# GAT layers with a residual layer norm: ScalarE's step tiles dealt anew in the first stage

## The chip, the cores and the metric

The kernel runs on one core of a Trainium2 chip. The time is the device time of one execution in microseconds (us). Five engines of the core run side by side, each through its own list of instructions in order, and wait for one another by semaphores: PE (TensorE, matrix products), DVE (VectorE), ACT (ScalarE), POOL (GpSimd) and SP (which here only starts transfers). The trace shows PE's weight loads apart, as PEld.

## The reference

Two graph attention layers on 512 nodes with 768 features, a residual and a layer norm. The graph has 16,896 edges (8,192 drawn pairs in both directions and a loop at each node), sorted by destination; an edge may occur more than once.

```python
def gat_layer(x, W, a_s, a_d, b, edge_index, concat):
    h = (x @ W).reshape(n, H, C)
    src, dst = (edge_index[0], edge_index[1])
    alpha_s = jnp.einsum('nhc,hc->nh', h, a_s)
    alpha_d = jnp.einsum('nhc,hc->nh', h, a_d)
    e = jax.nn.leaky_relu(alpha_s[src] + alpha_d[dst], NEG_SLOPE)
    m = jax.ops.segment_max(e, dst, num_segments=n)
    e = jnp.exp(e - m[dst])
    denom = jax.ops.segment_sum(e, dst, num_segments=n)
    alpha = e / (denom[dst] + EPS)
    msg = h[src] * alpha[:, :, None]
    out = jax.ops.segment_sum(msg, dst, num_segments=n)
...
h = gat_layer(x, W1, a_src1, a_dst1, b1, edge_index, concat=True)   # 8 heads
h = jax.nn.elu(h)
out = gat_layer(h, W2, a_src2, a_dst2, b2, edge_index, concat=True) # 1 head
return _layernorm(x + out)
```

## The kernel before

The kernel does not walk the edges. It counts them once, in `cnt`, a 512 x 512 table of how many edges lead from a source to a destination (and `absent`, a large negative number where there is none), and then does the attention of each head as dense 512 x 512 work. All large products are done in seven smaller ones of half the size instead of eight (the names `P1` to `P7`). The order of the instructions on every engine is written out by hand; no scheduler changes it.

**The first stage** (the first 63 us) does three things at once: the counting, the first projection `x @ W1` of head 0 (`first_projection`, fourteen products of three matmuls' depth, and the first four products of head 1), and the transposition of `x` on PE with copies of it by ACT (`turn_x`, line 205).

**The counting.** The edges are cut into 132 chunks of 128. For a chunk, DVE makes a narrow one-hot of the destinations within a block of 32 nodes (`od`, line 492, a quarter of the chunks at once), and one wide row per edge over all 512 sources (`os`, 128 x 512). A matmul of the two (line 542) adds the chunk to 32 rows of a counting tile in PSUM. The nodes make four tiles of 128 destinations. For three of them the wide row is a one-hot by DVE (line 516, `is_equal`). For tile `S = 2` it is a row of steps by ACT (line 514, the sign of `nodes - index`, with the negated index `nidx` as bias, which line 504 makes for all chunks): counting signs and taking the difference of neighbouring columns gives the same counts. That difference is the work of `counted_by_steps`: ACT reads the tile out of PSUM (lines 402 and 403), DVE subtracts (line 404), ACT makes `absent` (line 405). The other tiles are read out by `counted` (lines 395 and 396). A chunk on the border between tile 2 and its neighbour needs both kinds.

**The batches.** The chunks are dealt into nine batches, each with so many of the chunks outside tile 2 (`ours`) and so many inside it (`theirs`). The loop over the batches issues for batch n: DVE's one-hots (`sources`, with the subtractions of finished products in their middle, `waiting`), extra work (`extra`: the sums of x, the logits of head 0), then products until `wants[n]` are issued, each followed on ACT by the copy of its result (for products that only need a copy), by copies of `x` after the first and third product (`turns`), and by a `share` of the steps of batch n + 1 (`ahead`); and last the matmuls of batch n (`count`). The chunks of a batch go to four queues, one for each group of 32 rows, and are issued in turn; a few may stay over for the next batch. A tile whose chunks have all been counted is read out at the end of that `count`, before the next batch's instructions. After the last batch the logits are spread over the partitions by PE (`spread`), and the softmax of head 0 begins.

**The ring.** All wide rows, of DVE and of ACT, share the 32 buffers of `os`, given out in the order in which they are issued; an instruction that writes a buffer waits for the matmul that last read it.

The line numbers below are those of the kernel before; behind the first removed line the changed kernel's are one lower, and from the middle of the loop on two higher.

Of the kernel before, what the change touches and what calls it, by code (L numbers as in the profile page):

```python
# [13 lines left out]
AF = mybir.ActivationFunctionType  # L14
# [9 lines left out]
def kernel(tc: tile.TileContext, *args):  # L24


    with ExitStack() as ctx:
        flags = ctx.enter_context(tc.tile_pool(name="flags", bufs=1))
        ctx.enter_context(tc.manual_schedule())
        flag = flags.tile([1, 1], I32, name="flag")  # L30
        again = gat_pass(tc, flag, *args)
        with tc.If(again != 0):
            gat_pass(tc, None, *args)
# [3 lines left out]
def gat_pass(  # L37
# [16 lines left out]
    nc = tc.nc  # L54
# [145 lines left out]
    def turn_x(t, r):  # L200

        ps = mm.tile([P, 512], F32, name="mm")
        for k in range(HK):
            nc.tensor.transpose(ps[:, k * P:(k + 1) * P], x_sb[:, t, (r * HK + k) * P:(r * HK + k + 1) * P], ident)  # L204
        nc.scalar.copy(xT[:, r * HK:(r + 1) * HK, t * P:(t + 1) * P],
                       ps[:, :HALF].rearrange("p (k n) -> p k n", n=P))
# [4 lines left out]
    if general:  # L211
        nc.vector.tensor_copy(idx_f, idx_i)
        idx = ohp.tile([P, 2, EC], F32, name="idx")
# [6 lines left out]
    else:  # L220
# [41 lines left out]
        idx = ohp.tile([P, EC], F32, name="idx")  # L262
# [59 lines left out]
    def projection(h, XA, B_):  # L322

        HS[h] = hs = hpool.tile([P, NT, D], F32, name="hs")
        new_alpha(h)
        bank = {}
        tt = nc.vector.tensor_tensor

        def pair(p, i, start, empty):
            def multiply():  # L330
                if start:
                    bank[i] = mm.tile([P, 512], F32, name="mm")
                product(bank[i], XA, B_, p, i, start)
            return multiply, lambda: empty(i, bank[i][:, :HALF])

        steps = [
            ("P1", True, lambda i, ps: nc.scalar.copy(hs[:, 2 + i, L], ps)),
            ("P2", False, lambda i, ps: nc.scalar.copy(hs[:, i, L], ps)),
            ("P6", True, lambda i, ps: tt(hs[:, i, R], hs[:, 2 + i, L], ps, op=ALU.add)),
            ("P7", True, lambda i, ps: tt(hs[:, 2 + i, R], hs[:, i, R], ps, op=ALU.add)),  # L340
            ("P4", False, lambda i, ps: tt(hs[:, 2 + i, L], hs[:, i, R], ps, op=ALU.add)),
            ("P5", True, lambda i, ps: tt(hs[:, 2 + i, R], ps, hs[:, 2 + i, R], op=ALU.subtract)),
            ("P3", False, lambda i, ps: tt(hs[:, i, R], ps, hs[:, i, R], op=ALU.subtract)),
        ]
        return [pair(p, i, start, empty) for p, start, empty in steps for i in range(2)]
# [95 lines left out]
    def spread(h):  # L441
        pool, name = (bc, "bc") if h else (tr, "tr")
        BC[h] = pool.tile([P, 512], F32, name=name)
        for t in range(NT):
            nc.tensor.transpose(BC[h][:, t * P:(t + 1) * P],  # L445
                                AL[h][0][:, t:t + 1].to_broadcast([P, P]), ident)

    def lift(h, t):

        q = qpool.tile([P, N], F32, name="q")  # L450
        nc.scalar.activation(q, BC[h][:, :N], AF.Identity, bias=AL[h][1][:, t:t + 1], scale=-1.0)  # L451
        return q

    def leak(q):
        nc.vector.scalar_tensor_tensor(q, q, NEG_SLOPE, q, op0=ALU.mult, op1=ALU.min)

    def rank(q, t):

        nmax = small.tile([P, 1], F32, name="nmax")
        nc.vector.tensor_tensor_reduce(out=q, in0=q, in1=absent[:, t, :], scale=1.0, scalar=-NO_EDGE,  # L460
                                       op0=ALU.add, op1=ALU.min, accum_out=nmax)
        nc.scalar.activation(q, q, AF.Exp, bias=nmax, scale=-1.0)  # L462
        return q

    def turn_b1():
        psb = mm.tile([P, 512], F32, name="mm")
        nc.tensor.transpose(psb[:, :H * DC], b1_rows, ident[:H * DC, :H * DC])
        nc.scalar.copy(b1T, psb[:, :H * DC])
        nc.scalar.activation(nb1T, psb[:, :H * DC], AF.Copy, scale=-1.0)
# [4 lines left out]
    if not general:  # L474
# [15 lines left out]
        def destinations(lo, hi):  # L490
            lo, hi = at[lo], at[hi]
            nc.vector.tensor_tensor(od[:, lo:hi, :],  # L492
                                    rel[:, lo:hi].unsqueeze(2).to_broadcast([P, hi - lo, B]),
                                    nodes[:, :B].unsqueeze(1).to_broadcast([P, hi - lo, B]),
                                    op=ALU.is_equal)
# [5 lines left out]
            nc.vector.scalar_tensor_tensor(below, rel, 0.0, below, op0=ALU.is_ge, op1=ALU.mult, accum_out=found)  # L501

        nidx = ohp.tile([P, EC], F32, name="nidx")
        nc.scalar.activation(nidx, idx, AF.Copy, bias=0.5, scale=-1.0)

        def by_steps(b):
            return b * B // P == S
# [3 lines left out]
        def one_hot(c, steps):  # L511
            hot[c, steps] = o = ohp.tile([P, N], BF16, name="os", bufs=32)
            if steps:
                nc.scalar.activation(o, nodes, AF.Sign, bias=nidx[:, c:c + 1])  # L514
            else:
                nc.vector.tensor_scalar(o, nodes, idx[:, c:c + 1], None, op0=ALU.is_equal)  # L516

        def kinds(batch, steps):
            return [c for c in batch if any(by_steps(b) == steps for b in blocks[c])]

        def sources(chunks, between):

            for j, c in enumerate(chunks):
                if j == len(chunks) // 2:
                    for f in between:
                        f()
                one_hot(c, False)
# [37 lines left out]
        B1 = {}  # L565
        wants = [3, 4, 7, 10, 12, 14, 16, 18]
        batches = []
        for ours, theirs in ((16, 0), (8, 8), (8, 8), (12, 4), (12, 4), (12, 4), (13, 3), (14, 2), (4, 0)):
            take = [order[k][:m] for k, m in ((False, ours), (True, theirs))]
            del order[False][:ours], order[True][:theirs]  # L570
            batches.append(take[0][:ours // 2] + take[1] + take[0][ours // 2:])
        assert not any(order.values())
        pos, made, quarter, waiting = 0, set(), EC // NT, []
        for n, batch in enumerate(batches):
            for k in sorted({c // quarter for c in batch} - made):
                destinations(k * quarter, (k + 1) * quarter)
                made.add(k)
            sources(kinds(batch, False), waiting)
            ahead = kinds(batches[n + 1], True) if n + 1 < len(batches) else []
            items_here = max(wants[n] - pos if n < len(wants) else 0, 1)  # L580
            share = -(-len(ahead) // items_here)
            waiting = []
            for f in extra.pop(n, []):
                f()
            while n < len(wants) and pos < wants[n]:
                if pos == wholes:
                    pairs = projection(1, XA, B1)
                    items += [(m, e, False) for m, e in pairs[:4]]
                multiply, empty, on_vector = items[pos]
                multiply()  # L590
                if on_vector:
                    waiting.append(empty)
                else:
                    empty()
                pos += 1
                for t, r in turns.get(pos, []):
                    turn_x(t, r)
                for c in ahead[:share]:
                    one_hot(c, True)
                del ahead[:share]  # L600
            assert not ahead
            if n == 2:
                turn_b1()
            if n + 1 == len(batches):
                spread(0)
                q = [lift(0, t) for t in range(NT)]
                for t in range(NT - 1):
                    leak(q[t])
                for t in range(NT - 1):
                    rank(q[t], t)  # L610
            if n == 0:
                pst = mm.tile([P, 512], F32, name="mm")
                nc.tensor.matmul(pst[:1, :1], found, ones, start=True, stop=True)
            if n == 3:
                again = nc.values_load(flag[:1, :1], min_val=0, max_val=E)
            count(batch, n + 1 == len(batches))
# [460 lines left out]
```

## Time and profile before

| | |
|---|---|
| median of 4 runs | 653.74 us (653.34 to 654.59) |
| the profiled execution | 653.68 us, of which its span is 651.7 us |
| busy: PE, PEld | 640.9 us (98%), 398.3 us (61%) |
| busy: DVE, ACT, POOL | 506.9 us (78%), 273.8 us (42%), 49.0 us (8%) |
| mean granted clock of PE | 0.998 |
| wide one-hots by DVE, line 516 | 105, 344 to 354 ns each |
| rows of steps by ACT, line 514 | 39, 707 to 744 ns each |
| matmuls of the counting, line 542 | 210, 376 to 390 ns each, four groups side by side |

The span is the time from the first to the last instruction of the profiled execution. Instructions of an engine overlap a little at their ends, so the distance between the starts of two equal ones in a row is shorter than the length of one: sixteen one-hots of 0.35 us stand in 4.29 us. A matmul in fp32 is recorded as two.

The busy times by stretch of the first 82 us (us of the stretch in which each engine was busy):

| stretch, us | length | PE | DVE | ACT | granted clock |
|---|---|---|---|---|---|
| 0.00 to 21.66 | 21.66 | 19.60 | 17.61 | 15.39 | 1.00 |
| 21.66 to 42.73 | 21.07 | 20.77 | 19.00 | 13.88 | 1.00 |
| 42.73 to 59.70 | 16.97 | 16.97 | 16.73 | 8.71 | 1.00 |
| 59.70 to 62.73 | 3.03 | 2.16 | 2.36 | 2.26 | 1.00 |
| 62.73 to 82.00 | 19.27 | 19.27 | 17.63 | 13.57 | 1.00 |

### The profile page before, as it was taken

To read this page: it belongs to the slowest core of one execution; us is meant where nothing else is said; L and a number is where in the kernel's file an instruction comes from. 1 tells how busy PE (TensorE), PEld (TensorE's weight loads), DVE (VectorE), ACT (ScalarE), POOL (GpSimd) and SP (SyncE) were. 2 spreads that over 40 slices of the span, in tenths; PEclk is the share of its full clock that TensorE was granted. 3 is DMA by queue.
4 is the path that set the end of the run, shared out by engine and by line. 5 is a ranking of instruction groups with operands and counts; after the bars stand their busy time and mean duration, and the time that the engine had idled before them with its cause. 6 is when DMAs were issued, how large, how long until landed. Compare 5 with 4: busy or idle time off the path is not lost.

```text
span 651.7 us, 7058 instructions
## 1 busy us (share of the span) xinstructions
PE 640.9 (98%) x2347; PEld 398.3 (61%) x2347; DVE 506.9 (78%) x1102; ACT 273.8 (42%) x469; POOL 49.0 (8%) x90
## 2 busy tenths in 40 slices
PE   8999999999999999999999999999999999999995
PEld 5544586557755586557755586557755545645553
DVE  7989989968777777858777777858775588876775
ACT  6774744530736044531736054521736043243440
POOL 1320020011000010011000010011000000000000
PEclk9999999999999999999999999999999999999999
DMA  9993498196506790296506790296407865000122
GB/s 321 330 195 86 79 330 212 38 263 199 123 0 176 155 271 20 46 264 200 113 1 174 170 264 13 49 266 203 103 1 205 204 176 133 25 0 0 34 56 77
DMA packets 74186, 90.88 MB, mean 139 GB/s; under 512 B 36710, under 2 KB 58526, under 8 KB 74142
## 3 DMA queue, kind: packets, MB, share of 16 engines
q1 hardware_dynamic: 60478, 68.72, 33.6%
q0 software_dynamic: 12976, 20.65, 18.3%
q10 hardware_dynamic: 688, 0.98, 0.4%
q8 instruction: 20, 0.33, 0.2%
q14 instruction: 24, 0.20, 0.1%
HBM read 78.02 MB, written 1.57 MB: 122 GB/s over the span
## 4 chain that ended last, share of the span: by engine, by line
PE 96%; DVE 3%; issue 0%; ACT 0%; DVEq 0%
PE mm L304 64%; PE mm L763 17%; PE mm L709 6%; PE mm L1029 3%; PE held L304 2%; DVE os L516 1%; PE tr L542 1%; PE bc L177 1%; DVE odw L492 1%; PE bc L445 0%; PE bc L542 0%; PE tr L957 0%; PE tr L678 0%; PE mm L204 0%; DVE w1t L378 0%
## 5 line engine op out<-in xcount | busy, mean ns | idle before, releaser
L304 PE MATMUL mm<-w,gT 128*128 128x384 f32 x288 | 97.4, 487 | 0.0
L304 PE MATMUL mm<-w,xT 128*128 128x384 f32 x264 | 88.4, 488 | 0.0
L304 PEld LDWEIGHTS mm<-w,gT 128*128 128x128 f32 x288 | 53.9, 190 | 35.7 <-issue 2.0
L304 PEld LDWEIGHTS mm<-w,xT 128*128 128x128 f32 x264 | 49.8, 190 | 35.7 <-ACT os L514 0.8
L462 ACT ACTIVATE q<-q,nmax 128x512 f32<-128x512 f32 x36 | 25.8, 721 | 89.9 <-DVE nmax L460 89.9
L304 PE MATMUL mm<-w1t,gS 128*128 128x384 f32 x180 | 60.7, 486 | 0.0
L767 ACT COPY u<-mm 128x256 f32<-128x256 f32 x18 | 6.7, 372 | 119.3 <-PE mm L763 119.3
L304 PE MATMUL mm<-w2t,xS 128*128 128x384 f32 x168 | 56.6, 487 | 0.0
L763 PE MATMUL mm<-PT,hs 128*128 128x256 f32 x216 | 52.6, 379 | 0.0
L362 DVE TENSOR_TENSOR h<-h,mm 128x384 f32<-128x384 f32 x72 | 39.6, 551 | 14.4 <-PE mm L304 13.8
L304 PEld LDWEIGHTS mm<-w1t,gS 128*128 128x128 f32 x180 | 34.1, 190 | 23.6
L304 PEld LDWEIGHTS mm<-w2t,xS 128*128 128x128 f32 x168 | 31.8, 190 | 22.4 <-ACT q L451 0.4
L763 PEld LDWEIGHTS mm<-PT,hs 128*128 128x128 f32 x216 | 41.0, 190 | 7.2 <-issue 0.4
L686 ACT COPY nr<-q 128x1024 uint16<-128x1024 uint16 x32 | 33.4, 1044 | 23.2 <-DVE q L672 15.8
L709 PE MATMUL mm<-PT,hs 128*128 128x512 f32 x96 | 41.6, 593 | 0.0
L691 ACT COPY PT<-zr 128x1024 uint16<-128x1024 uint16 x32 | 37.1, 1159 | 2.0 <-DMA zr<-nr 2.0
L763 PE MATMUL mm<-pS,gS 128*128 128x256 f32 x144 | 37.1, 380 | 0.0
L304 PE MATMUL mm<-w,gS 128*128 128x384 f32 x96 | 32.6, 486 | 0.0
L304 PE MATMUL mm<-w1t,gT 128*128 128x384 f32 x96 | 32.5, 487 | 0.0
L304 PE MATMUL mm<-w,xS 128*128 128x384 f32 x96 | 32.5, 487 | 0.0
L106 POOL DMA_DIRECT2D w1t<-in_L_gnn_W_dram x7 | 8.9, 1267 | 312.5 <-PE mm L304 181.4
L709 PEld LDWEIGHTS mm<-PT,hs 128*128 128x128 f32 x96 | 18.2, 190 | 22.9 <-issue 21.5
(184 smaller groups left out, 1072.7 us busy)
## 6 DMA issues: line engine op xcount, KB each, us to landing
w<-in_L_gnn_W_dram SPq DMA_DIRECT2D x90, 384.0 KB, 6.1
w<-in_L_gnn_W_dram POOLq DMA_DIRECT2D x16, 576.0 KB, 9.7
w2t<-in_L_gnn_W_dram SPq DMA_DIRECT2D x10, 576.0 KB, 10.4
w1t<-in_L_gnn_W_dram SPq DMA_DIRECT2D x9, 576.0 KB, 4.4
w2t<-in_L_gnn_W_dram POOLq DMA_DIRECT2D x8, 576.0 KB, 10.0
w1t<-in_L_gnn_W_dram POOLq DMA_DIRECT2D x7, 576.0 KB, 8.5
a_s<-in_L_gnn_a_src_dram SPq DMA_DIRECT2D x8, 384.0 KB, 4.0
a_d<-in_L_gnn_a_dst_dram SPq DMA_DIRECT2D x8, 384.0 KB, 5.3
```

Of the source, the lines that this page charges most:

```text
L106: nc.gpsimd.dma_start(t1, upper[:, :, R], accum_op=ALU.add)
L177: nc.tensor.matmul(idle, zeros[:, :P], zeros, start=True, stop=True)
L304: nc.tensor.matmul(ps[:, :HALF], A_[p][:, k, i * P:(i + 1) * P], B_[p][:, k, :], start=start and k == 0, stop=k == HK - 1, skip_group_chec ...
L362: nc.vector.tensor_tensor(a, a, ps, op=ALU.subtract if p == "P7" else ALU.add)
L462: nc.scalar.activation(q, q, AF.Exp, bias=nmax, scale=-1.0)
L492: nc.vector.tensor_tensor(od[:, lo:hi, :], rel[:, lo:hi].unsqueeze(2).to_broadcast([P, hi - lo, B]), nodes[:, :B].unsqueeze(1).to_broadcas ...
L686: nc.scalar.copy(apart.rearrange("p (h n) -> p h n", h=2), q.bitcast(U16).rearrange("p (n h) -> p h n", h=2))
L691: nc.scalar.copy(PT.rearrange("p s n -> p (s n)").bitcast(U16).rearrange("p (s n h) -> p s n h", s=NT, h=2)[:, :, t * P:(t + 1) * P, :], p ...
L709: nc.tensor.matmul(ps[:, :N], HS[h][:, s, c * P:(c + 1) * P], PT[:, s, :], start=(s == 0), stop=(s == NT - 1))
L763: nc.tensor.matmul(bank[p][:, :HN], A_[p][:, k, c * P:(c + 1) * P], B_[p][:, k, :], start=over is None and k == 0, stop=k == 1, skip_group ...
L767: nc.scalar.copy(u, part("P1"))
L1029: nc.tensor.matmul(ps[:, :cols.stop - cols.start], PT[:, s, t * P:(t + 1) * P], h2[:, s, cols], start=(s == 2), stop=(s == 1))
```

## The change

```diff
@@ -501,7 +501,6 @@
         nidx = ohp.tile([P, EC], F32, name="nidx")
-        nc.scalar.activation(nidx, idx, AF.Copy, bias=0.5, scale=-1.0)
@@ -565,7 +564,7 @@
-        for ours, theirs in ((16, 0), (8, 8), (8, 8), (12, 4), (12, 4), (12, 4), (13, 3), (14, 2), (4, 0)):
+        for ours, theirs in ((16, 0), (8, 8), (8, 8), (12, 4), (12, 5), (12, 5), (13, 3), (14, 0), (4, 0)):
@@ -578,7 +577,7 @@
-            share = -(-len(ahead) // items_here)
+            share = len(ahead) // (items_here + 1) if n == 0 else -(-len(ahead) // items_here)
@@ -595,10 +594,13 @@
                 for t, r in turns.get(pos, []):
                     turn_x(t, r)
+                if pos == 1:
+                    nc.scalar.activation(nidx, idx, AF.Copy, bias=0.5, scale=-1.0)
                 for c in ahead[:share]:
                     one_hot(c, True)
                 del ahead[:share]
-            assert not ahead
+            for c in ahead:
+                one_hot(c, True)
```

- The negated indices are made behind the first product, its copy and two copies of `x`, instead of ahead of them.
- In batch 0, ACT makes two of batch 1's eight steps behind each of the three products (before: three, three and two), and the last two behind the four later copies of `x`.
- The two `theirs` of batch 7 are dealt to batches 4 and 5. In the order that is built, ACT then makes 8, 8, 4, 5, 9, 5 and 0 rows of steps for batches 1 to 7 (before: 8, 8, 4, 4, 8, 5 and 2), DVE makes 14 one-hots for each of batches 6 and 7 (before: 13 and 15), and the matmuls of counts 4 to 7 are 20, 34, 27 and 20 (before: 18, 32, 27 and 24). The numbers of all three kinds are the same in sum. Up to count 3, PE's and DVE's lists are the same, instruction for instruction.
- Tile 2 is complete with count 6 instead of count 7. `counted_by_steps` therefore stands one batch earlier in both lists: on ACT in front of the copies of head 1's second pair of products instead of behind them, on DVE in front of batch 7's one-hots and the logits of tile 3 instead of behind both.

## The prediction, made before the changed kernel was run

> **What bounds the kernel now.** I read the page's busy shares first (PE 98%), then the chain of waits, then the timelines of the first 63 us. The chain names the work that the end time hangs on, piece by piece (start, length, what):
>
> ```profile
> 20.74 0.87 DVE xS L284
> 21.61 0.04 issue
> 21.66 6.07 PE mm L304 x18
> ...
> 42.13 0.56 DVE hs L427
> 42.69 0.04 issue
> 42.73 4.14 PE held L304 x12
> ...
> 59.71 0.60 ACT steps L402
> ...
> 60.40 0.69 DVE cnt L404
> 61.09 1.06 DVE os L516 x4
> ...
> 62.81 19.55 PE mm L304 x60
> ```
>
> PE sets the end except in three places: up to 21.66 the chain runs through DVE alone (since 7.35), at 42.13 through one DVE subtraction, and from 59.71 to 62.20 through ACT's steps, DVE's difference and four one-hots (the last three matmuls of a count stand at 62.20, left out here). Behind 62.81 PE runs on without a break, so whatever moves that product moves the end by as much. The change touches all three places. DVE around the last two, and ACT and PE around the copies of x (timelines; start, length, and in brackets the idle time before, with its releaser):
>
> ```profile
> 39.73 1.14 DVE L516 TENSOR_SCALAR os<-nodes,idx 128x512 bf16<-128x512 f16 x4
> 41.60 0.62 DVE L516 TENSOR_SCALAR os<-nodes,idx 128x512 bf16<-128x512 f16 x2 [0.73 <-PE tr L542]
> 42.13 1.01 DVE L427 TENSOR_TENSOR hs<-hs,held 128x384 f32<-128x384 f32 x2
> ...
> 54.15 4.03 DVE L516 TENSOR_SCALAR os<-nodes,idx 128x512 bf16<-128x512 f16 x15
> 58.08 0.95 DVE L319 SCALAR_TENSOR_TENSOR scr<-hs,a_s 128x768 bf16<-128x768 f32 x1
> ...
> 60.40 0.69 DVE L404 TENSOR_TENSOR cnt<-steps 128x512 f32<-128x512 f32 x1 [0.35 <-ACT steps L403]
> 61.01 1.13 DVE L516 TENSOR_SCALAR os<-nodes,idx 128x512 bf16<-128x512 f16 x4
> ```
> ```profile
> 14.91 0.86 ACT L205 COPY xT<-mm 128x384 f32<-128x384 f32 x2
> 15.45 0.93 PE L204 MATMUL mm<-ident,hs 128*128 128x128 f32 x6 [0.56 <-ACT xT L205]
> ```
>
> From 42.13 to 60.05 DVE has no idle entry at all. It is full, though PE is the one on the chain.
>
> **Part one, the copies of x.** ACT makes two steps instead of three behind each of the first two products. One step costs 0.62 us from start to start (ten in 6.23). The negation (0.31) leaves a gap where ACT waited anyway (1.46 idle before 9.74) and now stands in the full stretch at 10.85. With it and two steps, ACT is free at 10.85 + 0.22 + 1.24 = 12.31, takes the second product's copy when that product ends (12.3 to 12.5), then two steps to about 14.1. The copies of the next transposes then start when their transposes are done: 14.07 + 0.58 = 14.65 (in the later pair, transposes at 15.45 and copy at 16.03, the distance is 0.58), against 14.91. PE gains 0.26 here, and keeps it through count 0, a product and count 1 up to the product at 21.66, which waits for the DVE sum xS that ends at 21.60. DVE's queue before it is the same instruction for instruction, has no idle time from 7.35 on, and waits for nothing that ACT now does earlier. So the gain becomes idle time of PE: 0 (bounds: 0 and -0.26, if DVE were not there). The other way: the four steps now left behind the copies end at 16.5 + 4 x 0.62 = 19.0, the first matmul of that tile is at 20.36; and twelve steps instead of ten end near 24.0, so the copy of 23.90 slips by 0.1, while the product that reuses its bank starts at 25.63. Both are covered by over 1 us. 0.
>
> **Part two, the ring of 32 one-hots.** Deals of 5 instead of 4 put ACT's five of batch 4 and nine of batch 5 (before: four and eight) into the ring ahead of DVE's thirteen of batch 5. In the built order of before, DVE's fifth and sixth one-hot of batch 5 wait for the first matmuls of count 4; that is the 0.73 idle ended by PE at 41.60. In the built order of after, the third to sixth do. PE's count 4 does not start earlier (everything on PE from 21.66 to 41.17 is the same). So four one-hots stand behind 41.60 instead of two, and behind them the subtractions L427: 41.60 + 4 x 0.266 = 42.66 instead of 42.13. The product at 42.73 waits for the first of these; it starts at 43.26, **+0.53**. Bounds: 0, if the slots come free earlier, and +0.8, if the fourth matmul of count 4, not the first, ends last.
>
> **Part three, the steps a batch sooner.** Counts 4 to 7 issue 20, 34, 27 and 20 matmuls instead of 18, 32, 27 and 24, at 0.064 each (32 in the 2.05 from 46.80 to 48.85). The steps' last matmul is now the last of count 6. PE's path to it: 43.26 + 4.07 (a pair of products) = 47.33; + 34 x 0.064 = 49.51; + 4.07 = 53.58; + 1.62 (27 matmuls, 52.92 to 54.54) = 55.20, its end 0.07 later, 55.27. From the end of that matmul to L404's start the chain shows 60.40 - 59.69 = 0.71, so L404 can start at 55.98. On ACT the steps stand in front of the copies of the next pair of products, the first of which ends near 57.3: covered. On DVE L404 has moved from behind the fourth pair of logits to in front of batch 7's fourteen one-hots. DVE reaches it at 54.15 + 0.53 + 0.26 (one more one-hot in batch 6) = 54.94, and stands for **1.04** us, where before it stood for 0.35. Queued behind it: fourteen one-hots, the logits of tile 3, four one-hots; PE's count 7, its spread and count 8 wait for these in that order. 55.98 + 0.61 (L404 to the next, 60.40 to 61.01) = 56.59; + 14 x 0.262 (15 in 58.08 - 54.15) = 60.26; + 1.89 (the pair of logits, 58.08 to 59.97) = 62.15, where the last four one-hots start, against 61.01. They lead to the next product as before: 62.73 - 61.01 = 1.72 later, 63.87. **+1.14** against 62.73. Bounds of this wait: none, if DVE arrives after 55.98 (then the four start at 61.11 and the sum is +0.10), and +0.4 more if the hand-over from PE through ACT takes half as long again.
>
> **Sum.** The removed stall (59.69 to 62.20) is not earned, because DVE, full on either side of it, must do the same pieces and now waits longer in a place where it was busy. The profiled execution took 653.68 (span 651.7 and 1.98 around it): 653.68 + 1.14 = 654.82. The median of the runs lies 0.06 higher, so 654.88. Nothing is moved past SP's or POOL's queue; the activation table is loaded once in this stage, before and after.
>
> **A rule on the clock.** In the stretch from 59.70 to 62.73 PE was idle for 0.74 us in one piece and the granted clock stayed 1.00. I add nothing for the clock. The Trainium skill (TensorE: Matmul & The Clock Gate, section "A second HAM failure mode: psum-queue depth-cycling") says that an array which idles briefly but often between groups of matmuls can have its clock swing between half and full. My estimate by the window of about 3.4 us that the same page gives (section "What's actually happening"): one window at half clock loses 1.7 us, and the time would be 656.6. No row here shows such a swing.
>
> **Rivals.**
> - *The gain arrives.* If DVE were not the bound, PE would go from 55.20 by 4.07, twenty matmuls (1.18), the spread (0.58) and count 8 (0.55) to 61.58: -1.15, 652.6; without the ring's wait (the product at 42.36) another -0.9, 651.7. For it: the chain does pass through the steps for 2.5 us. Against it: no idle entry on DVE from 42.13 to 60.05. It would need 2 us less work there.
> - *One of the two waits is not there.* Without the ring's wait the steps end 0.53 earlier: 654.4; without the wait at L404, 653.8. For it: idle entries are short and put down to the last of several semaphores. Against it: the built order names both.
> - *PE slows down too.* From 59.27 to 63.87 PE has 2.3 us of work (1.18 + 0.58 + 0.55) in 4.6. Should the granted clock fall to half there, the last 0.61 of count 8 and the first product (2.03) would take double: up to +2.6, half of it +1.3: 656.2. It decides from the point where the clock reads below 1. Against it: the row above.
>
> **How the numbers follow.** Forecast: 654.88, own range 654.4 to 655.6, chance 0.60. The gain arrives 0.10, one wait missing 0.11, slower PE 0.19. The range 653.7 to 656.0 leaves out the first rival and the upper half of the last. What a measurement can tell from no change is 0.2%, or 1.31: above 655.05 lie 0.27 of the forecast and the slower PE, 0.46; below 652.43 lies 0.08 (most of the first rival); within, 0.46.
>
> **What would show it.** Part one: PE's transposes at 15.2, with idle time in front of the product at 21.66 grown to about 0.4. Part two: four one-hots behind the wait at 41.60 and the product at 43.26. Part three: L404 near 56.0 with about 1.0 of idle time before it, the last four one-hots near 62.15, the product of 62.73 at 63.9. Wrong if L404 finds no wait, or if the product comes before 62.7.

## The result, and the profile after

| | before | after |
|---|---|---|
| median of the runs | 653.63 us (653.22 to 654.59, 60 runs) | 654.62 us (654.22 to 655.93, 40 runs) |
| the profiled execution, and its span | 653.68 us, 651.7 us | 654.33 us, 652.4 us |

The changed kernel takes 1.0016 times as long, with a 95% interval of 1.0011 to 1.0020: about 1.0 us more. That is less than the 0.2% which the forecast counted as no change, but the interval does not reach 1, so the small loss is there. The forecast of 654.88 us lies 0.26 us above the median.

First the chain of waits of the kernel after (start, length, what), at the places that were shown of before:

```profile
21.16 6.00 PE mm L304 x18
...
41.56 0.40 DVE os L515 x2
41.96 0.13 issue
42.09 0.56 DVE hs L427
42.65 0.04 issue
42.69 4.14 PE held L304 x12
...
54.65 0.60 ACT steps L402
...
55.34 0.69 DVE cnt L404
56.03 3.68 DVE os L515 x14
59.71 0.89 DVE scr L319 x2
...
61.59 1.07 DVE os L515 x4
...
63.30 19.55 PE mm L304 x60
```

Before, PE was off the chain for 2.5 us at the end of this stage. Now it is off from 54.65 to 62.69, over 8 us: behind ACT's steps the chain goes through DVE's difference, all fourteen one-hots of batch 7, the logits and the last four one-hots. The ring's wait is on it as well (41.56).

DVE's timeline of after at the two waits (start, length; in brackets the idle time before, with its releaser):

```profile
39.17 0.61 DVE L515 TENSOR_SCALAR os<-nodes,idx 128x512 bf16<-128x512 f16 x2
41.03 1.14 DVE L515 TENSOR_SCALAR os<-nodes,idx 128x512 bf16<-128x512 f16 x4 [1.25 <-PE tr L541]
42.09 1.01 DVE L427 TENSOR_TENSOR hs<-hs,held 128x384 f32<-128x384 f32 x2
...
55.34 0.69 DVE L404 TENSOR_TENSOR cnt<-steps 128x512 f32<-128x512 f32 x1 [0.89 <-ACT steps L403]
55.95 3.76 DVE L515 TENSOR_SCALAR os<-nodes,idx 128x512 bf16<-128x512 f16 x14
...
61.50 1.14 DVE L515 TENSOR_SCALAR os<-nodes,idx 128x512 bf16<-128x512 f16 x4
```

Four one-hots instead of two stand behind the ring's wait, and the difference waits in front of fourteen. The front, on PE and ACT:

```profile
7.40 2.17 PE L304 MATMUL held<-w,xT 128*128 128x384 f32 x6 [0.59 <-DMA w<-in_L_gnn_W_dram]
...
15.00 0.93 PE L204 MATMUL mm<-ident,hs 128*128 128x128 f32 x6 [0.24 <-ACT xT L205]
```

The later transposes wait for ACT's copies for 0.24 us instead of 0.56.

From the product behind the sums of x on, these times are about 0.6 us earlier than forecast, since that product starts at 21.09 instead of 21.66: the execution began differently (the first product waited for its weights here, while in the profile of before DVE was late), and the new front is shorter, as shown below. So every stretch below is counted from that product. PE's timelines at both ends of the stretch, before and after:

```profile
21.66 4.14 PE L304 MATMUL mm<-w1t,xS 128*128 128x384 f32 x12
...
62.74 4.14 PE L304 MATMUL mm<-w2t,xS 128*128 128x384 f32 x12
```
```profile
21.09 4.14 PE L304 MATMUL mm<-w1t,xS 128*128 128x384 f32 x12
...
63.23 4.14 PE L304 MATMUL mm<-w2t,xS 128*128 128x384 f32 x12
```

From the product behind the sums to the product behind the last four one-hots it is 62.74 - 21.66 = 41.08 us before and 63.23 - 21.09 = **42.14** us after, 1.06 more; behind that product the rest of the span is the same within 0.2 us (589.0 and 589.2).

### The profile page after: what moved, and what is told of

Read it like the earlier page. It is cut to its first block, busy times and chain, and to the rows that moved or that the text cites. A ratio compares the mean times of both kernels' runs of the same rounds, so it can differ in the third digit from the quotient of the medians.

```text
span 652.4 us, 7058 instructions
## 1 busy us (share of the span) xinstructions
PE 640.7 (98%) x2347; PEld 397.8 (61%) x2347; DVE 507.4 (78%) x1102; ACT 273.6 (42%) x469; POOL 47.6 (7%) x90
## 4 chain that ended last, share of the span: by engine, by line
PE 96%; DVE 2%; DMA 1%; ACT 0%; issue 0%; SPq 0%
PE mm L304 64%; PE mm L765 17%; PE mm L711 6%; PE mm L1031 3%; PE held L304 2%; PE tr L541 1%; DMA w<-in_L_gnn_W_dram 1%; DVE os L515 1%; PE bc L445 0%; PE bc L541 0%; PE tr L959 0%; DVE scr L319 0%; PE tr L680 0%; PE mm L204 0%; ACT xT L205 0%
## 5 line engine op out<-in xcount | busy, mean ns | idle before, releaser
L362 DVE TENSOR_TENSOR h<-h,mm 128x384 f32<-128x384 f32 x72 | 39.6, 551 | 14.3 <-PE mm L304 13.8
```

Source lines behind the costliest of these rows:

```text
L362: nc.vector.tensor_tensor(a, a, ps, op=ALU.subtract if p == "P7" else ALU.add)
```

## The experiments

Ten kernels ran, in three groups (the first four, the next four, the last two), each beside the kernel before (medians 653.70, 653.56 and 653.64 us). "Distance" is the stretch just defined. Where a kernel adds lines, its line numbers are up to two higher.

| kernel | time, us | ratio to before | distance, us |
|---|---|---|---|
| front alone | 653.53 | 0.9998 (0.9988 to 1.0007) | 41.08 |
| deal alone | 654.80 | 1.0017 (1.0007 to 1.0026) | 42.14 |
| after, 40 buffers | 653.62 | 0.9998 (0.9989 to 1.0007) | 41.45 |
| after, difference later | 653.61 | 0.9999 (0.9990 to 1.0008) | 41.21 |
| after, both | 651.92 | 0.9973 (0.9963 to 0.9984) | 39.80 |
| before, difference last | 652.53 | 0.9985 (0.9976 to 0.9994) | 40.08 |
| before, difference last, 40 buffers | 651.97 | 0.9975 (0.9965 to 0.9985) | 39.54 |
| after, difference last, 40 buffers | 651.78 | 0.9970 (0.9958 to 0.9982) | 39.55 |
| front alone, the same two edits | 651.74 | 0.9970 (0.9958 to 0.9982) | 39.54 |
| deal alone, the same two edits | 651.79 | 0.9971 (0.9959 to 0.9982) | 39.55 |

**The front alone.** The new place of the negation and the new share, with the old deal:

```diff
-        for ours, theirs in (..., (12, 4), (12, 5), (12, 5), (13, 3), (14, 0), (4, 0)):
+        for ours, theirs in (..., (12, 4), (12, 4), (12, 4), (13, 3), (14, 2), (4, 0)):
```

> Only the first part of the change (negation behind the first product, two steps instead of three per product in batch 0); the deal of the batches as before. Theory (the ring and the wait at the difference cost all): same as before within 0.2 us, 653.4 to 653.8; PE's second transposes start 0.3 to 0.45 us sooner after the first product than before, and the gap reappears in front of the first product that needs the sums of x, because DVE's list is not shorter. Rival (the front is earned, -0.26): 653.4 or less, product behind the sums 0.26 sooner counted from the first product. Second rival (the front costs the 1 us of the whole change): 654.6.

Measured 653.53 us, distance 41.08, as before's. The front is not where the loss comes from. One half of the theory missed: the second transposes do start 0.32 us sooner after the first product (15.38 - 7.78 = 7.60 against 15.45 - 7.53 = 7.92), but no gap reappears, and the product behind the sums stands 13.69 us behind the first product instead of 14.13. *The front*, further down, says why.

**The deal alone.** The new deal in the kernel before, nothing else:

```diff
-        for ours, theirs in (..., (12, 4), (12, 4), (12, 4), (13, 3), (14, 2), (4, 0)):
+        for ours, theirs in (..., (12, 4), (12, 5), (12, 5), (13, 3), (14, 0), (4, 0)):
```

> Only the deal of the batches of the change; the front as before. Theory: all of the loss, 654.6 (+1.0), with four one-hots behind the ring's wait and about 0.9 us of idle time in front of DVE's difference. Rival (the front costs it): 653.6.

Measured 654.80 us, 1.1 above the 653.70 beside it. Its DVE timeline has both waits, and the distance of after to the hundredth:

```profile
41.46 1.14 DVE L516 TENSOR_SCALAR os<-nodes,idx 128x512 bf16<-128x512 f16 x4 [1.26 <-PE tr L542]
...
55.77 0.69 DVE L404 TENSOR_TENSOR cnt<-steps 128x512 f32<-128x512 f32 x1 [0.89 <-ACT steps L403]
```

The whole loss is in the deal.

**After with a larger ring.**

```diff
-            hot[c, steps] = o = ohp.tile([P, N], BF16, name="os", bufs=32)
+            hot[c, steps] = o = ohp.tile([P, N], BF16, name="os", bufs=40)
```

> The whole change, with 40 buffers for the wide rows instead of 32: the ring's wait is gone, the wait in front of the difference stays. Theory (ring +0.5 and difference +0.6, one after the other): the product behind the subtractions starts where count 4 ends, 0.6 to 0.7 us sooner than in the changed kernel, and the time falls by as much, 653.9 to 654.0. Rival (the difference's wait alone sets the end and swallows the ring's): the idle time in front of the difference grows and the time stays at 654.6.

Measured 653.62 us, a little below what was expected: the time falls by 1.0, the distance by 0.69, and the 0.3 between them lies inside the interval. In DVE's timeline the six one-hots stand in one piece and the wait at the ring is gone, but the wait at the difference has grown from 0.89 to 1.55 us:

```profile
39.48 1.66 DVE L515 TENSOR_SCALAR os<-nodes,idx 128x512 bf16<-128x512 f16 x6
...
54.97 0.69 DVE L404 TENSOR_TENSOR cnt<-steps 128x512 f32<-128x512 f32 x1 [1.55 <-ACT steps L403]
```

DVE had 1.25 us of idle time to win. It keeps only what PE wins, since the difference waits for PE's count 6 through ACT, and PE wins 0.69: the product behind the subtractions stands 20.91 us behind the product behind the sums instead of 21.60. The rest of DVE's gain is handed to the next wait.

**After with the difference issued later**, behind batch 7's fourteen one-hots instead of in front of them (`absent` behind batch 7's products on ACT):

```diff
+    late = []
...
-        nc.vector.tensor_tensor(cnt[:, t, :], steps[:, 1:], steps[:, :N], op=ALU.subtract)
-        nc.scalar.activation(absent[:, t, :], cnt[:, t, :], AF.Relu, bias=far, scale=NO_EDGE)
+        late.append(lambda: nc.vector.tensor_tensor(cnt[:, t, :], steps[:, 1:], steps[:, :N], op=ALU.subtract))
+        late.append(lambda: nc.scalar.activation(absent[:, t, :], cnt[:, t, :], AF.Relu, bias=far, scale=NO_EDGE))
...
             sources(kinds(batch, False), waiting)
+            if n == 7:
+                late.pop(0)()
...
             for c in ahead:
                 one_hot(c, True)
+            if n == 7:
+                late.pop(0)()
```

> The whole change, with DVE's difference (and ACT's absent behind it) issued behind batch 7's fourteen one-hots instead of in front of them; 32 buffers. Theory: the 0.9 us of idle time in front of the difference is gone, the ring's wait stays; the time falls by 0.8 to 0.9 to 653.7 to 653.8. Rival (the ring's delay alone is the loss): 654.6 as in the changed kernel. Second rival (PE was not waiting for DVE there): the idle time moves to another place and less than 0.3 is won.

Measured 653.61 us, distance 41.21, 0.93 less than after's. DVE's timeline shows the fourteen one-hots going ahead and the difference with no idle entry:

```profile
54.64 3.76 DVE L517 TENSOR_SCALAR os<-nodes,idx 128x512 bf16<-128x512 f16 x14
58.31 0.69 DVE L406 TENSOR_TENSOR cnt<-steps 128x512 f32<-128x512 f32 x1
```

The wait of 0.89 at L404 was thus of after's own making: the input came too late for the new place.

**Both edits at once.**

> Both waits of the changed kernel taken away at once: 40 buffers, and DVE's difference behind batch 7's fourteen one-hots. Theory (DVE sets the end between 42 and 62 us and the two waits stand one behind the other on it): the savings add. From the product behind the sums to the product behind the last four one-hots, 40.5 us (41.21 with the later difference alone, less the 0.69 that the larger ring gave by itself); time 652.9, below before by 0.7 to 0.8. Rival (PE sets the end once one wait is gone): the second removal brings nothing, 653.6, the distance stays at 41.2.

Measured 651.92 us and 39.80. The savings don't just add: 0.69 and 0.93 alone, 42.14 - 39.80 = **2.34** together. Both theories missed. DVE's lost time in after accounts for it, counted at each wait from where the next instruction could have started to where it did: from 39.17 + 2 x 0.262 = 39.69 to 41.03 at the ring, 1.34, and from 54.36 to 55.34 at the difference, 0.98, in sum 2.32. Removed alone, the later wait gave nearly all of its 0.98. The earlier one gave only half of its 1.34, because the later one, left in place, swallowed the rest. Removed together, DVE runs through:

```profile
53.58 3.76 DVE L517 TENSOR_SCALAR os<-nodes,idx 128x512 bf16<-128x512 f16 x14
57.26 0.68 DVE L406 TENSOR_TENSOR cnt<-steps 128x512 f32<-128x512 f32 x1
```

**Before with the difference behind the last four one-hots.** The same lists `late`, popped for batch 8: the difference behind the four one-hots, `absent` behind the four `lift`s.

> The kernel before, with its old deal, but DVE's difference of the steps behind the last four one-hots instead of in front of them. Theory (DVE sets the end there): the four start where the fourth pair of logits ends, 60.05 instead of 61.01, and the product behind them moves by 0.96: distance from the product behind the sums 40.1, time 652.7. Rival (the difference is needed as early by what follows, the softmax of head 0): the product comes 0.96 earlier, but PE waits later in the softmax for the same 0.96, time 653.7.

Measured 652.53 us, distance 40.08: both as the theory had it (652.7, 40.1). Nothing that follows needed the difference earlier.

**The same with 40 buffers.**

> The same with 40 buffers. Theory: the 0.73 us of DVE's wait in the ring goes too, of which the product in the middle shows 0.37: distance 39.4 to 39.7, time 652.0 to 652.4. Rival (the old deal's ring wait costs nothing, since only two one-hots stand behind it): distance 40.1, time 652.7.

Measured 651.97 us, distance 39.54: the time is at the favourable end of the theory, the distance in its middle. So, with the difference out of the way, the old deal's ring wait cost 0.54 us too. The larger ring alone in the kernel before was not run.

**After with these two edits.**

> The changed kernel with 40 buffers and the difference behind the last four one-hots. Theory: as with 40 buffers and the difference behind batch 7's one-hots, less the difference's own 0.6 us: distance 39.9, time 652.3. Against the kernel before with the same two edits (652.0 to 652.4) the new deal is then worth nothing either way. Rival (the new deal frees PE, and shows its gain once DVE's waits are gone): 651.7, 0.5 below the other.

Measured 651.78 us, distance 39.55. It is half a microsecond faster than expected, but the old deal with the same edits has the same distance, 39.54, so the rival's gain from the new deal is not there. The busy times of the stretch (its length, then the busy time and count of PE, PEld, DVE, ACT and POOL, PE's granted clock, DMA share, GB/s) say why. Before (to 62.73, where the product's weights begin to load), after, and after with the two edits:

```profile
21.66:62.73 41.07, 39.89 (x253) 20.23 (x253) 38.09 (x107) 24.86 (x47) 9.97 (x7) 1.00 0.79 188
```
```profile
21.09:63.23 42.14, 40.30 (x257) 20.35 (x253) 38.97 (x108) 27.29 (x51) 8.48 (x7) 1.00 0.77 182
```
```profile
21.57:61.12 39.55, 39.55 (x254) 20.15 (x254) 37.77 (x107) 25.01 (x47) 9.37 (x7) 1.00 0.81 194
```

PE is busy in 39.89 of 41.07 us before, in 40.30 of 42.14 after, and in all of the 39.55 with the two edits. Busy time holds short waits between matmuls as well: the twenty of count 7 stand in 1.59 us in after (at 58.57) and in 1.26 here, though one is 0.38 us long in both. With the two edits PE has no idle time left in this stretch, with the old deal (39.54 busy of 39.54) as with the new. The same matmuls must run in any deal, so once DVE's waits are gone the deal has nothing left to bring. It is also why moving the difference behind the last four one-hots brought only 0.25 us (39.80 to 39.55), and not its own 0.6 as expected.

**The set completed**, the front alone and the deal alone with the same two edits.

> Old deal, new front (negation behind the first product, two steps behind each of the three), with 40 buffers and the difference behind the last four one-hots. Theory one: the front is worth a little wherever the first product waits for its weights (from there to the product behind the sums 13.69 us with the new front against 14.01 with the old), and the new deal is worth nothing (distance from the product behind the sums to the one behind the last one-hots 39.54 with the old deal, 39.55 with the new): 651.8, distance 39.5. Theory two (the front is worth nothing, the 0.2 between the two kernels with both edits comes from the new deal): 652.0.

> New deal, old front, with the same two edits: the fourth of the set. Theory one: 652.0, from the first product to the one behind the sums 14.0 (or more, where DVE starts late), distance from there 39.55. Theory two (the new deal brings the 0.2): 651.8.

Measured 651.74 and 651.79 us, distances 39.54 and 39.55; from the first product to the product behind the sums it is 13.70 and 14.01 us, as theory one had it. The distances confirm that the deal is worth nothing once the waits are gone. On the front the times of the four kernels with 40 buffers and the difference last decide nothing: they lie within 0.23 us of one another, and the interval of each is 1.3 to 1.6 us wide.

Every kernel without the two waits beats the kernel before and the kernel after. The smallest change is to leave the deal and the front as they were, give the ring 40 buffers and issue the difference last: 0.9975 (0.9965 to 0.9985).

## Why the prediction was right

*The ring's wait.* Forecast: the product behind the subtractions 43.26 - 21.66 = 21.60 behind the product behind the sums. Measured: 42.69 - 21.09 = 21.60. It was +0.53 by reading how many one-hots stand behind the wait. Shown by the deal alone and by the larger ring.

*The wait at the difference.* Counted from the same product, DVE was to arrive at 33.28 and start at 34.32; it arrived at 54.36 - 21.09 = 33.27 and started at 55.34 - 21.09 = 34.25. The last four one-hots start at 40.41 instead of the forecast 40.49, the next product at 42.14 instead of 42.21. Forecast +1.14, measured +1.06. Shown by the deal alone, and by issuing the difference later.

*The front.* This is the one term that holds only in part. Worth 0 was argued from the profile of before, where the product behind the sums waits for DVE. In the traces of all twelve kernels that product stands either 14.3 us behind DVE's start on the indices (L261, 7.35 before), or 14.0 us (old front) or 13.7 us (new front) behind the first product, whichever is later:

| | L261 | first product | product behind the sums | counted from |
|---|---|---|---|---|
| before | 7.35 | 7.53 | 21.66 | L261, 14.31 |
| after, both | 7.36 | 7.51 | 21.66 | L261, 14.30 |
| deal alone | 6.63 | 7.51 | 21.52 | first product, 14.01 |
| after | 6.70 | 7.40 | 21.09 | first product, 13.69 |
| front alone | 6.81 | 7.78 | 21.47 | first product, 13.69 |

Where DVE is late, the gain becomes idle time of PE exactly as forecast (0.40 us there, in the row "after, both"). In nine of the twelve profiled executions the first product came last instead, behind its weights, and there the new front is 0.32 us shorter. So in these profiles the bound of -0.26 was the usual case and the 0 the rarer one: one profiled execution of before had shown the rare one. In the times it is not resolved: the front alone is 0.17 us below before, and the whole change costs 0.99 where the deal alone costs 1.10, each against the kernel before beside it; both lie well inside the intervals. The change in time, less the change in distance, is -0.07 to -0.45 us in the seven kernels with the new front and +0.04 to -0.32 in the four with the old: a hint at a gain, no more.

One size in part one was also off, without consequence: the negation was put at 0.22 us in ACT's list and took 0.37 (10.72 to 11.09), but ACT still waited 0.44 us for the transposes behind it.

*The 0.26 us that are left.* The forecast started from 653.74, the median of four runs of before; that of sixty is 653.63. That is 0.11 of the 0.26 by which it was too high. The wait's size is another 0.08 (1.14 against 1.06). For the last 0.07 no cause was shown. The forecast put the front at nothing, and most profiles show 0.32 us there; that this did not move the time further from the forecast was not explained, and is luck as far as is known.

*The rivals.* Missing waits: both were there. The slower PE: no sign of it. The twelve matmuls behind the gap take 4.14 us, like the twelve at 54.51 behind none:

```profile
54.51 4.14 PE L304 MATMUL mm<-w,xT 128*128 128x384 f32 x12
...
61.91 1.40 PE L541 MATMUL tr<-os,odw 128*32 128x512 bf16 x8 [0.94 <-DVE os L515]
63.23 4.14 PE L304 MATMUL mm<-w2t,xS 128*128 128x384 f32 x12
```

The gain that arrives: it did not, for the reason given, but the reason held one wrong sentence. The forecast said that DVE "would need 2 us less work there". It needed no less work: the kernel after with 40 buffers and the difference last has the same instructions on DVE and reaches 651.78, where the forecast's figure for this rival was 651.7. It is not the change that brings it, since the old deal with these edits has the same distance. What stood in the way were the two waits, 2.34 us, and the place of the difference, 0.25, in sum 42.14 - 39.55 = 2.59. A DVE without an idle entry from 42.13 to 60.05 looked full; it was also behind, by the wait just ahead of that stretch.

## What to carry to other kernels

An engine that takes its instructions in order charges a wait to everything queued behind the waiting one. Making an input earlier did not pay here, because its consumer moved up with it, to a place where the input was not ready yet and in front of fourteen one-hots that did not need it; moving the consumer down, in the old kernel, was worth 1.0 us.

Of two waits that follow one another on one engine, the later one can hide the earlier: the ring's wait alone brought 0.69 of its 1.34 us. Take away both before calling the earlier one small.

Read starts of stages from more than one execution, and count from an instruction that both kernels share.

## What was not expected of the hardware

The first microseconds differ between executions by more than the front is worth, and PE is part of it. The six first transposes, of before and of before with the difference last:

```profile
5.01 1.49 PE L204 MATMUL mm<-ident,hs 128*128 128x128 f32 x6
```
```profile
4.74 0.82 PE L204 MATMUL mm<-ident,hs 128*128 128x128 f32 x6
```

The same work takes 1.49 or 0.82 us. PE does not wait within it: each matmul is 421 or 273 ns long, and their starts are 0.21 or 0.11 us apart. The next six of before, at 9.54, take 0.82, and the granted clock reads 1.00 in all these stretches. The transposes of the indices follow, and DVE's L261 waits for them: 7.35 and 6.21. The Trainium skill (TensorE: Matmul & The Clock Gate, section "What's actually happening") says that the array runs at half clock until it has been busy for a window of about 3.4 us, and that the window runs free of the program. PE's first matmul is at 1.19 in both traces. The transposes are at the shorter length from 4.74, 3.55 us later, in the one, and not yet at 5.01, 3.82 us later, in the other; with a window that can begin later this agrees, but that the gate is the cause was not tried. It follows that the granted clock of 1.00, which the forecast put against the slower PE, was not the right witness, since it reads 1.00 here too; a slow row stood in before's own profile, where the forecast saw none. The lengths of the matmuls are the witness.
